# Adaptive-layernorm block in float32 on one core: summing eight factors in the DMA instead of on GpSimd, with a rearranged start

## The chip, the cores and the metric

The kernel runs on 1 core of one Trainium2 chip. The metric is device time in microseconds (us) of one execution; the median of three executions of the kernel before is 536.98 us (536.24 to 539.12). Engine names are those of the profile: PE is TensorE (PEld its weight loads), DVE is VectorE, ACT is ScalarE, POOL is GpSimd, SP is the sync engine, which here only issues DMAs.

## The reference, cut to what matters

Four batches `b` of 1024 tokens with 512 channels go through one attention block and one linear block, each behind a layer norm whose scale, shift and gate come from a small conditioning vector. All is float32.

```python
mod = (silu(c) @ wmod)            # 6 rows of 512 per batch: sa, ca, ga, sb, cb, gb
ga, gb = sign(.) * max(|.|, 0.25) of their rows
h = layernorm(x) * (1 + ca) + sa
# attention: every one of the 16 heads has the same scores, of rank 64
scores = (h Wq^T)(h Wk^T)^T;  attn = softmax(scores)
x = x + ga * ((attn @ (h Wv^T)) @ Wo^T)
h = layernorm(x) * (1 + cb) + sb
# the linear block: eight 512 x 512 factors act as their sum
x = x + gb * (h @ sum_r factors[r] / sqrt(8) + bias)
```

Since all heads share one attention matrix, the kernel multiplies the value and output weights into one matrix first (`wvo`), and since the linear block is linear in the factors, it sums the eight factors once (`fsum`).

## The kernel before, in words

**Stages.** For the first batch there is a start: load weights and tokens, multiply `wv` and `wo` into `wvo` (L172), make the modulation rows (L189), normalize the first batch's tokens and transpose them on PE (L375), and project queries and keys (L398, tile `ps_qk`). Then each batch runs: scores and `y = h·wvo·ga` alternating tile by tile (L425 and L478), the product of probabilities and `y` (L517), and, interleaved with the next batch, the linear block (L542). A batch has 8 token tiles of 128; `p` counts pairs of tiles, 4 a batch.

**The product.** Probabilities times `y` goes by a scheme with seven half-size products per pair (`n` = 1 to 7) in place of eight. It needs sums and differences of quarters of the transposed probabilities (`sum_probs`, L464, DVE) and of quarters of `y` (`sum_y`, L488; on DVE for batch 0). Each product of a pair is added into the residual tile `x` by one DVE instruction (`add`, L531), and products share PSUM banks: 1, 6, 7 and 4 accumulate in a bank `y` (two of these exist), 5 and 3 in `q`, 2 in `x`. So product 6, which goes on in the bank of product 1, cannot start before DVE has added product 1.

**Transposes.** Probabilities (128x2048 for a pair) are transposed in 32x32 blocks on DVE (`turn_probs`, L450, one instruction a pair), and 16 DMAs on SP's queue then move the blocks to their partitions (`move_probs`, L455, through `move_blocks`, L325). Normalized tokens go the same way (`turn_h`, `move_h`).

**Factors.** `fsum` receives factor 0 by two DMAs. Factors 1 to 7 are loaded in halves of 512 KB to one buffer of two halves (`load_factor`, L251) and added by POOL (`add_factor`, L267), 14 loads and 14 adds. POOL's queue issues both. POOL also computes reciprocal standard deviations (`rstd`, L300), parts of the second gate (L228), the scaled weights `w` of batches 1 to 3 (L276), the scaled `f` (L281), `sum_y` of batches 1 to 3, and it adds the bias rows to the residual (`add_bias`, L554). Stores of batches 0 to 2 and loads of the later batches' tokens are issued on its queue too.

**What sets the order.** A `Plan` (L17) holds every piece of work with a beat, written by hand; `pe(n, ...)` takes n beats of PE's time, `at(beat, ...)` puts other work beside it. Pieces are issued in order of beat, and each engine and queue runs its own list strictly in that order. A beat of the product stage is about 0.43 us: 112 beats there take 48 us. In the plan of batch 0, the score stage begins at beat 84, the product stage at 168, and the layer norm of batch 1's second half asks POOL for its standard deviations at beat 204.

**PSUM.** Eight banks: `y` has two tiles of one bank, `sc` two tiles of two banks, `q` and `x` one each. `psum_mm` (L91) hands out y, q, y, x in turn when no tag is given.

**First loads.** Before: the chunks of `wv`, the four first token tiles and the modulation weights go on SP's queue; `cT` (8 KB, the conditioning vector) and the four chunks of `woT` go on ACT's queue, `cT` first.

Of the kernel before, what the change touches and what calls it, by code (L numbers as in the profile page):

```python
# [12 lines left out]
ALU = mybir.AluOpType  # L13
# [3 lines left out]
class Plan:  # L17
# [6 lines left out]
    def at(self, beat, fn, *args):  # L24
        self.work.append((beat, len(self.work), fn, args))

    def pe(self, beats, fn, *args):
        self.at(self.now, fn, *args)
        self.now += beats
        return self.now  # L30
# [7 lines left out]
def kernel(  # L38
# [17 lines left out]
    nc = tc.nc  # L56
    P = 128
    B, T, D = x.shape
    NR = factors.shape[0]
    R = wqkT.shape[1] // 2  # L60
    KC = D // P
    NT = T // P
    NP = NT // 2
    GT = NT // 2
# [3 lines left out]
    NQ = P // Q  # L68
# [10 lines left out]
    wfp = ctx.enter_context(tc.tile_pool(name="wfp", bufs=2))  # L79
# [6 lines left out]
    def psum(tag, width, name):  # L86
        return psp.tile([P, width], F32, tag=tag, bufs=2 if tag in ("y", "sc") else 1, name=name)
# [3 lines left out]
    def psum_mm(name, tag=None):  # L91
        turn[0] += 1
        return psum(tag or "yqyx"[turn[0] % 4], 512, name)

    plan = Plan()
    at, pe = plan.at, plan.pe
# [15 lines left out]
    def load_x(b, t, queue=nc.sync):  # L112
        xt[b, t] = xp.tile([P, D], F32, tag="x", name=f"x_{b}_{t}")
        queue.dma_start(out=xt[b, t], in_=x[b, ts(t, P), :])

    def wide(pool, tag, name):
        return pool.tile([P, KC, D], F32, tag=tag, name=name)

    wvs, wos = wide(prp, "pr", "wvs"), wide(prp, "pr", "wos")
# [3 lines left out]
    def load_wmod(m):  # L123
        nc.sync.dma_start(
            out=wms[m], in_=wmod[:, ts(m, D)].rearrange("(kc p) e -> p kc e", p=P)
        )

    wqk = const.tile([P, KC, 2 * R], F32, name="wqk")
    cTs = const.tile([P, KC, B], F32, name="cTs")

    def load_weights(cc):
        nc.sync.dma_start(out=wvs[:, cc, :], in_=wv[ts(cc, P), :])
        nc.scalar.dma_start(out=wos[:, cc, :], in_=woT[ts(cc, P), :])

    for cc in range(KC - 1):
        load_weights(cc)
        load_x(0, cc)
        if cc == 0:
            nc.scalar.dma_start(out=cTs, in_=cT.rearrange("(kc p) b -> p kc b", p=P))
    load_x(0, KC - 1)  # L140
    load_wmod(0)
    load_wmod(1)
    load_weights(KC - 1)
# [20 lines left out]
    wvo = const.tile([P, KC, D], F32, name="wvo")  # L164
    pw = [psum("sc", T, f"ps_wvo_{h}") for h in range(2)]
# [6 lines left out]
    def wvo_chunk(cc, kcs=range(KC)):  # L172
        for kc in kcs:
            nc.tensor.matmul(  # L174
                pw[kc // 2][:, ts(kc % 2, 512)], wvs[:, cc, ts(kc, P)], wos[:, cc, :],
                start=(cc == 0), stop=(cc == KC - 1),
            )
        if cc == KC - 1:
            for kc in kcs:
                nc.scalar.copy(wvo[:, kc, :], pw[kc // 2][:, ts(kc % 2, 512)])  # L180

    row_tiles = [sp.tile([B, 3, D], F32, tag="s", name=f"rows_{h}") for h in range(2)]

    def row(m):
        return row_tiles[m // 3][:, m % 3, :]

    chans, rows_d, ps_mod = {}, {}, {}

    def mod_products(ms):  # L189
        ps = psum_mm(f"ps_mod_{ms[0]}", "q")  # L190
        for kc in range(KC):
            for g, m in enumerate(ms):
                nc.tensor.matmul(  # L193
                    ps[32 * g : 32 * g + B, :], scT[:, kc, :], wms[m][:, kc, :],
                    start=(kc == 0), stop=(kc == KC - 1),
                )
        for g, m in enumerate(ms):
            ps_mod[m] = ps[32 * g : 32 * g + B, :]
# [47 lines left out]
        nc.tensor.matmul(bcs["ga", 0], sel, row(2), start=True, stop=True)  # L246

    fsum = const.tile([P, KC, D], F32, name="fsum")
    fac = {}

    def load_factor(n):  # L251

        r, half = divmod(n, 2)
        if n == 0:
            fac["buffer"] = wide(wfp, "wf", "factors")
        f = fac["buffer"][:, ts(half, KC // 2), :]
        if r == 0:
            f = fsum[:, ts(half, KC // 2), :]
            nc.gpsimd.tensor_copy(f[0:1, 0, 0:1], chans[1][0:1, 0, 0:1])
        elif r == 1:  # L260
            nc.gpsimd.tensor_copy(f[0:1, 0, 0:1], chans[1][0:1, 0, 0:1])
        fac[n] = f
        nc.gpsimd.dma_start(
            out=f, in_=factors[r, ds(half * D // 2, D // 2)].rearrange("(kc p) e -> p kc e", p=P)
        )

    def add_factor(n):  # L267
        k = ts(n % 2, KC // 2)
        nc.gpsimd.tensor_tensor(fsum[:, k, :], fsum[:, k, :], fac[n], ALU.add)  # L269

    wb, fb = {}, {}

# [52 lines left out]
    def move_blocks(src, dst, apart, queue=nc.sync):  # L325

        if apart:
            src = src.rearrange("p (c n e) -> p c n e", c=NQ, e=Q)
            dst = dst.rearrange("p (n r e) -> p r n e", r=NQ, e=Q)
        else:  # L330
            src = src.rearrange("p (c w) -> p c w", c=NQ)
            dst = dst.rearrange("p (r w) -> p r w", r=NQ)
        for r in range(NQ):
            for c in range(NQ):
                queue.dma_start(out=dst[ts(c, Q), r], in_=src[ts(r, Q), c])  # L335

    def turn_h(ln, b, g, c):
# [57 lines left out]
    def project(b, g):  # L395
        if g == 0:
            qkT[b] = (
                qkp.tile([2 * R, T], F32, tag="qT", name=f"qT_{b}"),  # L398
                qkp.tile([2 * R, T // 2], F32, tag="kT", name=f"kT_{b}"),
            )  # L400
        ps = psum_mm(f"ps_qk_{b}_{g}")
        for kc in range(KC):
            nc.tensor.matmul(  # L403
                ps[: 2 * R, :].rearrange("p (r w) -> p r w", r=NQ), wqk[:, kc, :],
                h1_chunk(b, g, kc),
                start=(kc == 0), stop=(kc == KC - 1),
            )
        ps_qk[b, g] = ps
# [14 lines left out]
    probs, ps_sc, den, rinv, PT, S = {}, {}, {}, {}, {}, {}  # L423
# [23 lines left out]
            AF.Exp, bias=nm, scale=1.0, accum_out=den[b, p][:, k : k + 1],  # L447
        )

    def turn_probs(b, p):  # L450
        nc.vector.reciprocal(rinv[b][:, 2 * p : 2 * p + 2], den[b, p])  # L451
        v = probs[b, p].rearrange("p c k j e -> p (c k j e)")
        nc.vector.transpose(v, v)  # L453

    def move_probs(b, p):  # L455
# [103 lines left out]
    def plan_softmax(b, p, k):  # L559

        at(plan.now + 0.5, exponents, b, p, k)
        if k:
            at(plan.now + 7, turn_probs, b, p)
            at(plan.now + 8, move_probs, b, p)

    def plan_start():
        for g in range(2):
            s = 8.0 if g == 0 else 44.0
            for j in range(GT):
                at(s + 2 * j, stats, 1, 0, g * GT + j)  # L570
            at(s + 9, rstd, 1, 0, g)
            for j in range(GT):
                at(s + 10 + j, normalize_first, g * GT + j)
        pe(8, warm_up)
        for cc in range(KC - 1):
            pe(8, wvo_chunk, cc)
        pe(8, mod_products, [0, 1])
        at(plan.now, mod_row, 1, nc.vector)
        at(plan.now, mod_row, 0, nc.scalar)
        pe(4, wvo_chunk, KC - 1, range(2))  # L580
        for m, plus in ((1, 1.0), (0, 0.0)):
            pe(1, channel_products, m)
            at(plan.now, channel, m, plus)
        pe(4, wvo_chunk, KC - 1, range(2, KC))
        for kc in range(KC):
            pe(1, turn_first, 0, kc)
            at(plan.now, first_out, 0, kc)
        for n in range(2 * NR):
            at(plan.now + 10 * max(0, n - 3), load_factor, n)
            if n >= 2:  # L590
                at(plan.now + 10 * max(0, n - 1), add_factor, n)
        pe(8, project, 0, 0)
        at(plan.now, qk_out, 0, 0)
        for kc in range(KC):
            pe(1, turn_first, 1, kc)
            at(plan.now, first_out, 1, kc)
        pe(8, mod_products, [2, 3, 4, 5])
        at(plan.now, mod_row, 2, nc.vector)
        for m in (3, 4, 5):
            at(plan.now, mod_row, m, nc.scalar)  # L600
        at(plan.now, gate, 2)
        at(plan.now, publish, row(2), "ga")
        pe(8, project, 0, 1)
        at(plan.now, qk_out, 0, 1)
        pe(2, spread_first)
        for kc in range(KC):
            at(plan.now, scale_w, 0, kc, nc.vector)
# [43 lines left out]
    def plan_ln2(b, g, ready):  # L651

        for j in (GT - 2, GT - 1):
            at(ready, stats, 2, b, g * GT + j)
        at(ready + 0.5, rstd, 2, b, g)
        for j in range(GT):
            at(ready + 5 + 2 * j, normalize, 2, b, g, j, nc.vector)
        for c in range(NQ):
            at(ready + 13 + 2 * c, turn_h, 2, b, g, c)
        at(ready + 19.5, move_h, 2, b, g)  # L660
        for j in range(GT):
            at(ready + 16, add_bias, b, g * GT + j)
        for kc in range(KC):
            at(ready + 55, shift_h, 2, b, g, kc, nc.scalar)

# [92 lines left out]
```

## Time and profile before

| | before |
|---|---|
| median of 3 executions | 536.98 us (536.24 to 539.12) |
| profiled execution: time | 538.23 us |
| its span, first to last instruction | 536.4 us |
| PE idle in the span | 16.0 us (536.4 less 520.4 busy) |
| PE idle from 97.7 to 532.7 us | 0.07 us |
| DVE busy | 347.6 us, 65% of the span |
| POOL busy | 198.0 us, 37% |
| POOL's 14 factor adds (L269) | 33.4 us, 2388 ns each |
| POOL's 32 bias additions (L555) | 43.9 us, 1394 ns each |
| mean granted TensorE clock | 0.986 |
| HBM read, written | 28.33 MB, 8.41 MB |

The profiled execution is 1.25 us above the median; 1.83 us of its time lie outside its span. A row of the view by stages gives, for each stretch of time, the busy time and the number of instructions of PE, PEld, DVE, ACT and POOL, then the clock granted to TensorE (1.00 is full), the mean busy share of the 16 DMA engines, and GB/s. The share can pass 1, since a packet's time includes waiting. In a row of the timeline the two first numbers are start and duration in us; what stands in brackets is the idle time before the instruction and what ended it. L numbers are lines of the kernel.

### The profile page before, as it was taken

The page shows a single profiled execution, that of the slowest core. Times are in us where ns is not written, and L with a number is a line of the kernel's source. Part 1 is how long each engine was busy: PE and PEld are TensorE (multiplying, and loading weights), DVE is VectorE, ACT ScalarE, POOL GpSimd, SP SyncE. Part 2 cuts the span into 40 slices and gives each one's busy share as a digit, 9 for nine tenths or more (in the row PEclk, how much of TensorE's full clock was granted, in tenths as well). Part 3 has the DMA queues.
Part 4 walks back from the last instruction along what each step waited for, and adds up shares of the span by engine and source line. Part 5 has one row for each costly group of instructions (what it writes and reads, how often), then busy time and mean ns, then how long its engine had stood idle before and what let it go on. Part 6 is the DMA issues. An engine that isn't in the chain of part 4 may idle for free.

```text
span 536.4 us, 5575 instructions
## 1 busy us (share of the span) xinstructions
PE 520.4 (97%) x1738; PEld 306.6 (57%) x1738; DVE 347.6 (65%) x568; ACT 131.5 (25%) x206; POOL 198.0 (37%) x170
## 2 busy tenths in 40 slices
PE   8988998799999999999999999999999999999997
PEld 4343334688743344888743344888743348887442
DVE  3448699899765546689665545789665673784611
ACT  1133322212255410222155310232155310001020
POOL 1038487563144162243145072244144060450600
PEclk9997999799999999999999999999999999999999
DMA  9993589864537679523536679423536677005352
GB/s 321 381 388 116 146 156 216 139 132 106 77 51 106 93 138 227 166 69 79 78 50 104 98 148 226 155 64 80 78 50 110 96 130 139 6 5 76 102 134 78
DMA packets 223342, 68.60 MB, mean 128 GB/s; under 512 B 206528, under 2 KB 207040, under 8 KB 223312
## 3 DMA queue, kind: packets, MB, share of 16 engines
q1 hardware_dynamic: 216704, 48.30, 46.9%
q0 software_dynamic: 5504, 18.88, 10.9%
q10 hardware_dynamic: 1104, 1.06, 0.6%
q8 instruction: 14, 0.23, 0.2%
q14 instruction: 16, 0.13, 0.1%
HBM read 28.33 MB, written 8.41 MB: 68 GB/s over the span
## 4 chain that ended last, share of the span: by engine, by line
PE 88%; DVE 4%; SPq 2%; DMA 2%; ACT 2%; issue 1%; ACTq 0%; DVEq 0%
PE ps_o_y L526 21%; PE ps_f L545 20%; PE ps_y L483 17%; PE ps_o_q L526 10%; PE ps_sc L430 6%; PE ps_o_x L526 5%; PE ps_qk L403 5%; PE ps_wvo L174 3%; SPq L335 2%; PE ps_mod L193 1%; DMA wos<-in_woT_dram 1%; DMA pt<-pr 1%; DVE s L472 1%; DVE pr L453 1%; ACT hT L387 1%
## 5 line engine op out<-in xcount | busy, mean ns | idle before, releaser
L483 PE MATMUL ps_y<-w,hT 128*128 128x512 f32 x256 | 119.2, 609 | 0.0
L545 PE MATMUL ps_f<-f,hT 128*128 128x512 f32 x256 | 110.5, 592 | 0.0
L483 PEld LDWEIGHTS ps_y<-w,hT 128*128 128x128 f32 x256 | 46.8, 192 | 69.2 <-issue 67.6
L545 PEld LDWEIGHTS ps_f<-f,hT 128*128 128x128 f32 x256 | 48.6, 190 | 60.8 <-issue 59.6
L300 POOL TENSOR_TENSOR r<-v,mhalf 128x4 f32<-128x4 f32 x16 | 18.0, 1126 | 148.0 <-DVE v L298 130.9
L354 ACT ACTIVATE hT<-hT,chan,chan 128x512 f32<-128x512 f32 x56 | 41.0, 805 | 116.1 <-DMA hT<-st 116.1
L526 PE MATMUL ps_o_y<-y,pt 128*128 128x256 f32 x256 | 58.5, 379 | 0.0
L549 DVE TENSOR_TENSOR x<-ps_f,x 128x512 f32<-128x512 f32 x32 | 21.9, 685 | 50.7 <-PE ps_f L545 50.7
L526 PEld LDWEIGHTS ps_o_y<-y,pt 128*128 128x128 f32 x256 | 48.6, 190 | 8.3 <-issue 1.9
L293 DVE BATCH_NORM_STATS2 bn<-x 128x6 f32<-128x512 f32 x64 | 43.3, 677 | 6.7 <-DMA x<-in_x_dram 6.7
L555 POOL TENSOR_TENSOR x<-x,bc_gbias 128x512 f32<-128x512 f32 x32 | 43.9, 1394 | 6.1 <-DVE st L319 5.4
L317 ACT ACTIVATE st<-x,m,r 128x512 f32<-128x512 f32 x24 | 17.6, 803 | 112.1 <-DVE m L305 72.5
L443 DVE TENSOR_REDUCE nm<-ps_sc 128x1 f32<-128x1024 f32 x32 | 38.3, 1206 | 5.6 <-PE ps_sc L430 5.6
L534 DVE SCALAR_TENSOR_TENSOR x<-ps_o_y,ri,x 128x256 f32<-128x256 f32 x64 | 30.2, 471 | 17.6 <-PE ps_o_y L526 17.4
L281 POOL TENSOR_TENSOR f<-fsum,bc_gb 128x512 f32<-128x512 f32 x16 | 20.7, 1324 | 54.7 <-DMA bc_gb<-rows_gb 54.7
L444 ACT ACTIVATE pr<-ps_sc,nm 128x1024 f32<-128x1024 f32 x32 | 35.7, 1117 | 19.9 <-DVE nm L443 15.6
L339 DVE STREAM_TRANSPOSE st<-st 128x512 f32<-128x512 f32 x56 | 37.0, 689 | 5.5 <-ACT st L317 5.2
L430 PE MATMUL ps_sc<-kT,qT 64*128 64x512 f32 x128 | 38.8, 663 | 0.0
L453 DVE STREAM_TRANSPOSE pr<-pr 128x2048 f32<-128x2048 f32 x16 | 36.9, 2306 | 2.6 <-DMA pt<-pr 1.7
L269 POOL TENSOR_TENSOR fsum<-fsum,factors 128x1024 f32<-128x1024 f32 x14 | 33.4, 2388 | 11.7 <-DMA factors<-in_factors_dram 11.6
L526 PE MATMUL ps_o_y<-yt,s 128*128 128x256 f32 x128 | 32.1, 396 | 5.0 <-DVE x L534 5.0
L451 DVE RECIPROCAL ri<-den 128x2 f32<-128x2 f32 x16 | 2.6, 165 | 52.5 <-ACT pr L444 52.5
(81 smaller groups left out, 633.2 us busy)
## 6 DMA issues: line engine op xcount, KB each, us to landing
pt<-pr SPq DMA_DIRECT2D x256, 64.0 KB, 2.3
hT<-st SPq DMA_DIRECT2D x224, 64.0 KB, 2.2
factors<-in_factors_dram POOLq DMA_DIRECT2D x14, 512.0 KB, 5.1
wm<-in_wmod_dram SPq DMA_DIRECT2D x6, 1024.0 KB, 9.7
out_dram<-x POOLq DMA_DIRECT2D x24, 256.0 KB, 3.5
x<-in_x_dram SPq DMA_DIRECT2D x16, 256.0 KB, 8.9
x<-in_x_dram POOLq DMA_DIRECT2D x16, 256.0 KB, 4.6
out_dram<-x SPq DMA_DIRECT2D x8, 256.0 KB, 2.0
```

What stands on the lines that cost most here:

```text
L269: nc.gpsimd.tensor_tensor(fsum[:, k, :], fsum[:, k, :], fac[n], ALU.add)
L293: nc.vector.bn_stats(s, xt[b, t])
L339: nc.vector.transpose(s, s)
L354: eng.activation(v, v, AF.Identity, bias=shift, scale=scale)
L430: nc.tensor.matmul(ps_sc[b, i][:, ts(h, 512)], qT[h * R : (h + 1) * R, ts(i, P)], kT[h * R : (h + 1) * R, :], start=True, stop=True,)
L443: nc.vector.tensor_reduce(nm, ps_sc[b, i], AX.X, ALU.max, negate=True)
L444: nc.scalar.activation(probs[b, p][:, :, k].rearrange("p c j e -> p j c e"), ps_sc[b, i].rearrange("p (j c e) -> p j c e", j=NT, c=NQ), AF ...
L453: nc.vector.transpose(v, v)
L483: nc.tensor.matmul(ps, h_rows(1, b, t, kc), wb[b][:, kc, :], start=(kc == 0), stop=(kc == KC - 1))
L526: nc.tensor.matmul(ps, a[:, ts(j, P)], bb[:, j, :], start=(tag is not None and j == 0), stop=(j == GT - 1), skip_group_check=tag is None,)
L545: nc.tensor.matmul(ps, h_rows(2, b, t, kc), fb[b][:, kc, :], start=(kc == 0), stop=(kc == KC - 1))
L555: nc.gpsimd.tensor_tensor(xt[b, t], xt[b, t], bcs["gbias", b], ALU.add)
```

## The change

- **Factors.** The eight factors go into `fsum` by eight DMAs of 1 MB on POOL's queue; the first writes, the other seven add to what is there. Each waits for the one before, since they write one tile. The buffer, the 16 half loads and the 14 POOL adds are gone. The eight are issued at beats 54, 78, ... 222 in place of 54 to 194.
- **Bias additions** move from 16 beats after the second layer norm's ready point to 76 and 36 beats after it (24 in the last batch), 4 beats apart: for batches 0 to 2 they fall into the next batch's score stretch.
- **First loads.** All `wv` and `wo` chunks go on SP's queue; the first four token tiles go on ACT's, with `cT` behind them.
- **PSUM and weight copies.** The first batch's projection uses `sc` tiles; the products of modulation rows 2 to 5 use a `y` tile, not `q`. Copies of `wvo` out of PSUM are placed singly; the last two come behind the first layer-norm copies on ACT's list. As `psum_mm` is called without a tag less often, the turn of the later tiles moves by two.
- **Turnings in pieces.** `turn_probs` transposes a pair in four pieces of 128x512, 1.6 beats apart, and `move_blocks` issues its 16 DMAs piece by piece. `move_probs` stands 12 beats after the scores in place of 8.

```diff
     def load_weights(cc):
         nc.sync.dma_start(out=wvs[:, cc, :], in_=wv[ts(cc, P), :])
-        nc.scalar.dma_start(out=wos[:, cc, :], in_=woT[ts(cc, P), :])
+        nc.sync.dma_start(out=wos[:, cc, :], in_=woT[ts(cc, P), :])
     for cc in range(KC - 1):
         load_weights(cc)
-        load_x(0, cc)
-        if cc == 0:
-            nc.scalar.dma_start(out=cTs, in_=cT.rearrange("(kc p) b -> p kc b", p=P))
-    load_x(0, KC - 1)
+        load_x(0, cc, nc.scalar)
+    load_x(0, KC - 1, nc.scalar)
+    nc.scalar.dma_start(out=cTs, in_=cT.rearrange("(kc p) b -> p kc b", p=P))
...
-        if cc == KC - 1:
-            for kc in kcs:
-                nc.scalar.copy(wvo[:, kc, :], pw[kc // 2][:, ts(kc % 2, 512)])
+    def wvo_out(kc):
+        nc.scalar.copy(wvo[:, kc, :], pw[kc // 2][:, ts(kc % 2, 512)])
...
-    def load_factor(n):
...
-    def add_factor(n):
-        k = ts(n % 2, KC // 2)
-        nc.gpsimd.tensor_tensor(fsum[:, k, :], fsum[:, k, :], fac[n], ALU.add)
+    def sum_factor(r):
+        if r == 0:
+            nc.gpsimd.tensor_copy(fsum[0:1, 0, 0:1], chans[1][0:1, 0, 0:1])
+        nc.gpsimd.dma_start(
+            out=fsum, in_=factors[r].rearrange("(kc p) e -> p kc e", p=P),
+            accum_op=ALU.bypass if r == 0 else ALU.add,
+        )
...
-        for r in range(NQ):
-            for c in range(NQ):
+        for c in range(NQ):
+            for r in range(NQ):
                 queue.dma_start(out=dst[ts(c, Q), r], in_=src[ts(r, Q), c])
...
-        ps = psum_mm(f"ps_qk_{b}_{g}")
+        ps = psum_mm(f"ps_qk_{b}_{g}") if b else psum("sc", T, f"ps_qk_{b}_{g}")[:, :512]
...
-    def turn_probs(b, p):
-        nc.vector.reciprocal(rinv[b][:, 2 * p : 2 * p + 2], den[b, p])
-        v = probs[b, p].rearrange("p c k j e -> p (c k j e)")
+    def turn_probs(b, p, c):
+        if c == 0:
+            nc.vector.reciprocal(rinv[b][:, 2 * p : 2 * p + 2], den[b, p])
+        v = probs[b, p][:, c].rearrange("p k j e -> p (k j e)")
         nc.vector.transpose(v, v)
...
-            at(plan.now + 7, turn_probs, b, p)
-            at(plan.now + 8, move_probs, b, p)
+            for c in range(NQ):
+                at(plan.now + 7 + 1.6 * c, turn_probs, b, p, c)
+            at(plan.now + 12, move_probs, b, p)
...
+        at(plan.now, wvo_out, 2)
+        at(plan.now, wvo_out, 3)
+        for r in range(NR):
+            at(plan.now + 24 * r, sum_factor, r)
...
-        pe(8, mod_products, [2, 3, 4, 5])
+        pe(8, mod_products, [2, 3, 4, 5], "y")
...
-            at(ready + 16, add_bias, b, g * GT + j)
+            at(ready + (24 if b + 1 == B else 76 if g == 0 else 36) + 4 * j, add_bias, b, g * GT + j)
```

More of the change, by code (lines that the diff above doesn't have):

```diff
@@ L187, with mod_products @@
     chans, rows_d, ps_mod = {}, {}, {}
-    def mod_products(ms):
-        ps = psum_mm(f"ps_mod_{ms[0]}", "q")
+    def mod_products(ms, tag):
+        ps = psum_mm(f"ps_mod_{ms[0]}", tag)
         for kc in range(KC):
@@ L248 @@
     fsum = const.tile([P, KC, D], F32, name="fsum")
-    fac = {}
-    def load_factor(n):
[L253 to L256, printed above, removed]
-        if r == 0:
[L258 to L262, printed above, removed]
+    def sum_factor(r):
+        if r == 0:
+            nc.gpsimd.tensor_copy(fsum[0:1, 0, 0:1], chans[1][0:1, 0, 0:1])
         nc.gpsimd.dma_start(
-            out=f, in_=factors[r, ds(half * D // 2, D // 2)].rearrange("(kc p) e -> p kc e", p=P)
-        )
-    def add_factor(n):
-        k = ts(n % 2, KC // 2)
-        nc.gpsimd.tensor_tensor(fsum[:, k, :], fsum[:, k, :], fac[n], ALU.add)
+            out=fsum, in_=factors[r].rearrange("(kc p) e -> p kc e", p=P),
+            accum_op=ALU.bypass if r == 0 else ALU.add,
+        )
     wb, fb = {}, {}
@@ L576, in plan_start @@
             pe(8, wvo_chunk, cc)
-        pe(8, mod_products, [0, 1])
+        pe(8, mod_products, [0, 1], "q")
         at(plan.now, mod_row, 1, nc.vector)
@@ L580, in plan_start @@
         pe(4, wvo_chunk, KC - 1, range(2))
+        at(plan.now, wvo_out, 0)
+        at(plan.now, wvo_out, 1)
         for m, plus in ((1, 1.0), (0, 0.0)):
@@ L587, in plan_start @@
             at(plan.now, first_out, 0, kc)
[L588 to L591, printed above, removed]
+        at(plan.now, wvo_out, 2)
+        at(plan.now, wvo_out, 3)
+        for r in range(NR):
+            at(plan.now + 24 * r, sum_factor, r)
         pe(8, project, 0, 0)
```

## The prediction, on record before the result

> **What bounds the kernel now.** I read the page's first part, then the busy time by stages cut where PE's idle time changes, then the waits and the chain that ended last, then the timeline of 38 to 98 us. PE is busy in 97% of the span, so the question is where the other 16.0 us lie. The view by stages (start:end, then length, busy PE, PEld, DVE, ACT, POOL, clock, DMA share, GB/s):
>
> ```profile
> 18.50:29.50 11.00, 9.85 (x49) 4.40 (x48) 5.76 (x15) 4.15 (x7) 1.10 (x2) 1.00 1.05 386
> 29.50:46.50 17.00, 13.92 (x66) 5.71 (x66) 9.49 (x13) 4.84 (x9) 8.08 (x11) 1.00 0.73 271
> 46.50:56.30 9.80, 9.80 (x19) 3.31 (x18) 6.38 (x10) 1.93 (x4) 8.85 (x7) 0.65 0.44 155
> 56.30:88.40 32.10, 32.10 (x89) 12.72 (x90) 28.31 (x35) 10.89 (x19) 21.02 (x15) 1.00 0.85 166
> 88.40:97.70 9.30, 3.90 (x18) 2.79 (x16) 9.30 (x15) 1.68 (x3) 2.90 (x2) 0.85 1.12 192
> 97.70:532.70 435.00, 434.93 (x1472) 269.97 (x1472) 281.24 (x462) 106.48 (x164) 154.35 (x130) 1.00 0.53 103
> ```
>
> From 97.7 us on PE never waits, at full clock: nothing done there to DVE, POOL or SP can save time. All that can be won lies before 97.7 us, and the largest piece is the stretch from 88.4, where DVE is busy all 9.30 us and PE 3.90. The waits name it:
>
> ```profile
> PE ps_o_y L526 <- DVE x L534: 5.0, 1, 5.0
> ```
>
> Product 6 waits for DVE's addition of product 1. The timeline shows why DVE is late (start, length, engine, line):
>
> ```profile
> 84.84 2.33 POOL L269 TENSOR_TENSOR fsum<-fsum,factors 128x1024 f32<-128x1024 f32 x1 [0.55 <-DMA factors<-in_factors_dram]
> 84.90 2.83 DVE L472 TENSOR_TENSOR s<-pt 128x512 f32<-128x512 f32 x1 [0.19 <-DMA pt<-pr]
> ...
> 88.21 2.36 POOL L269 TENSOR_TENSOR fsum<-fsum,factors 128x1024 f32<-128x1024 f32 x1
> ...
> 88.78 2.08 DVE L499 TENSOR_TENSOR yt<-y,yt 128x256 f32<-128x256 f32 x1
> ...
> 91.46 0.68 DVE L472 TENSOR_TENSOR s<-s,pt 128x512 f32<-128x512 f32 x1
> ```
>
> The same DVE instruction takes 2.83 us when a POOL factor add is running and 0.68 us when none is: it ends just after POOL's add ends. DVE stands still while POOL adds.
>
> **Part 1, the POOL adds go.** In the stretch before the addition of product 1, four DVE instructions run into POOL adds: 128x1024 at 78.49 (2.04 us, POOL until 79.44: 0.85 lost), 128x256 at 80.97 (2.58 against 0.41: 2.17), 128x512 at 84.90 (2.83 against 0.68: 2.15), 128x256 at 88.78 (2.08 against 0.41: 1.67). Sum 6.8 us. The wait is 5.04; it goes if DVE keeps pace. What is then late next is PE itself: DVE's addition would come near 97.12 - 6.8 = 90.3, and product 5 ends at 92.6. PE's clock also fell in that wait: product 6 took 3.78 us against 1.73 for its kind later, 2.05 more, and the next 0.2 more. Value -7.2, from 0 (something else holds DVE) to -7.2.
>
> Earlier, the gate's instruction L221 takes 2.45 us at 42.27, beside a POOL add from 41.84 to 44.45, and 0.41 at 65.20, without one. It is on the chain: row 2, gate, `ps_ga`, where PE waits 1.47. With 2.04 off, PE's own projection is last there: -1.47. The clock of 0.65 in 46.5 to 56.3 follows that gap: eight `ps_y` records take 5.02 us there against 3.70 later, 1.3 more, and the eight `ps_sc` 4.79 against 2.30 in batch 1, of which 1.5 is the wait for `scale_w`, which stays, so 1.0 more. I take -1.5 of the 2.3, since one gap of three stays; bounds 0 to -2.3.
>
> **Part 2, banks.** PE waits 0.87 before the first projection (bank q, until ACT has copied the fourth transposed chunk), 0.67 before a transpose (bank q again, L421), 0.87 before the modulation products (again). Other banks are free there: -2.4. The limit is the modulation weights: the last of six 1 MB loads is issued at 18.1 and lands 13.5 later, at 31.6; with parts 2 and 3 it is wanted at 36.78 - 2.4 - 1.5 = 32.9. So the cover is 1.3 us; without it part 2 is 0. A changed turn gives product 5 bank q without the wait for `y`'s copy: -0.36.
>
> **Part 3, first loads.** PE's warm-up ends at 5.00 and the first `wvo` product starts at 6.41, when the first `wo` chunk lands (1.23 + 5.05 on ACT's queue). In front of it there sits `cT`, which ACT had only at 3.94 although it has 8 KB. The first token tile, issued at 1.18 behind one 256 KB chunk on SP's queue, landed by 4.34. That is the place that `wo` gets, but it now shares the engines with token tiles. Lower end: it lands as the second `wv` chunk did (1.65 + 5.1 = 6.76 for the third in the queue, so no gain). Upper end: 1.41 and the 1.7 us that four cold records at 0.85 cost over 0.43, -3.1. Value -1.5, nearer to the token tile's row.
>
> **Part 4, pieces.** A 128x2048 turning takes 2.31 us; two 128x512 together 1.29 in `turn_h`, so four cost 2.6: +0.3 a pair, 1.2 before the addition, inside the 2.3 us by which DVE is early (92.6 - 90.3). The first moves can start after one piece, 1.6 us sooner (0.69 against 2.31); they are issued at 0.67 us each alone (10.80 for 16), 0.80 beside factor loads (38.54 for 48).
>
> **Part 5, bias additions.** 32 POOL instructions of 1.39 us leave the product stage (DVE 34.4 of 40 us busy in 220:260) for the score stage (23.1 of 40 in 260:300). PE has no idle time in either: 0. The cover is DVE's 17 idle us per 40. In POOL's list they stand around `scale_f`, which waits 13.96 us for its broadcast row and ends at 173.5; `ps_f` begins at 189.1. Bounds 0.
>
> **Part 6, the new wait.** POOL blocks at each summing DMA until the one before has landed. Behind it stand, for batch 0: the second gate (and through it two SP DMAs, ahead of pair 1's moves), and `rstd` for batch 1 at beats 171 and 204, the latter behind the seventh sum. The profile has no such DMA. Low bound: a half load alone, 3.6 us. High: four half loads one after another at the slowest under moves, 4 x 6.0 = 24 us, since each 1 MB must also be read where it is added. I take 12: two half loads under moves are 10.4 (2 x 5.2), plus something for the second read. Condition: before, the second `rstd` at 114.02 was 24.2 us ahead of the finished shift at 138.25, and the projection took that at 148.2. With PE 14.5 earlier, `rstd` may come at 148.2 - 14.5 - 24.2 = 109.5. The fourth sum is held to about 62 by the gate, so the seventh goes out at 62 + 3D: at D = 12, 98, and 0 cost. From D = 16 PE waits; from 20.5 the whole gain is gone.
>
> The Trainium skill ("Collectives: The Full Stack", The bandwidth ceiling) says that a DMA which adds reads two sources and reached about half the rate of a copy. No run here shows it yet; applied to the 5.2 row it gives about 2 x 2 x 3.2 + 2 = 15 us, an estimate, and the sum stays as it is.
>
> The same skill ("SBUF — State Buffer", Two separate sides) speaks against DMAs from POOL: DVE's two-port modes keep POOL from writing descriptors. The trace does not show it for the factor loads: 14 issues at 0.72 to 0.78 us, most beside a busy DVE. By the rule each sum might start up to a DVE instruction later; the sum above has no term for it.
>
> **Give-back.** SP's moves now set when DVE can form `sum_probs`. With PE 6.9 earlier at the first exponents, SP starts near 52; pair 0 ends near 64; at 0.80 each pair 2 lands near 64 + 25.6 + 4.4 = 94 against a need near 92, pair 3 near 107 against 104. DVE runs in order, so its additions wait a little: +2 (0 to +6).
>
> **Sum.** -7.2 - 1.5 - 1.5 - 2.4 - 0.4 - 1.5 + 2 = -12.5 from 538.23: 525.7; from the median, 1.25 lower, 524.5. I say 525. All favourable ends: -7.2 - 1.5 - 2.3 - 2.4 - 0.4 - 3.1 = -16.9, 520 from the median.
>
> **Rivals.** (a) *Moves late.* Each 0.1 us more per move issue is 4.8 us on pair 3. At 0.90 the give-back is 2 + 5: about 531. For: the DMA share is already 1.12 there. Against: the sums come one at a time, with gaps. (b) *The gain given back whole*: at 1.05 per issue, 12 us, 537, no change. (c) *Slower: the sums take too long.* At D = 24 the seventh goes out at 134, 25 us past 109.5: 525 + 25 = 550. It decides from D = 20.5. For: nothing in the profile excludes it; against: the half loads' 3.6 to 6.0 us.
>
> **Chances.** Forecast 0.62, (a) 0.20, (b) 0.07, (c) 0.11. About 0.5% (2.7 us) is what a measurement of this kernel tells from no change: faster 0.82, same 0.07, slower 0.11. The range 520 to 533 holds the forecast with its bounds and (a).
>
> **What would show it.** No POOL adds, and 128x512 and 128x256 sums on DVE at 0.68 and 0.41 from 75 to 95; the wait of `ps_o_y` on DVE under 1; clock 1.00 in that stretch; `wvo` starting near 5; the sums landing within 16 us. A wait of PE on `ps_qk` near 135, or of DVE on `pt` near 95, would make the prediction wrong.

## The result, and the profile after

The changed kernel takes 553.1 us (median of four, 548.3 to 553.6) against 536.6 for the kernel before on the same chip: a ratio of 1.028 (95% interval 1.021 to 1.035). It is slower; 525 was predicted, with a range of 520 to 533. The profiled execution took 553.6 us, with a span of 551.8 and a mean clock of 0.978.

The view by stages of the changed kernel, with the same columns as before (start:end, length, busy PE, PEld, DVE, ACT, POOL, clock, DMA share, GB/s):

```profile
46.50:56.30 9.80, 9.80 (x21) 3.98 (x20) 4.11 (x8) 2.84 (x5) 1.29 (x1) 0.77 0.67 115
88.40:97.70 9.30, 6.39 (x22) 5.34 (x23) 5.42 (x14) 2.93 (x4) 2.68 (x2) 0.82 0.62 88
110.00:120.00 10.00, 10.00 (x48) 8.81 (x47) 5.70 (x14) 2.93 (x4) 1.50 (x2) 1.00 0.99 161
120.00:130.00 10.00, 2.62 (x9) 1.89 (x8) 2.87 (x5) 0.00 (x0) 1.20 (x1) 0.80 0.92 171
```

From 88.4 to 97.7 us PE now works 6.39 us instead of 3.90, as intended. But from 120 to 130 us, where it had no idle time before, it stands for 7.4 of 10 us, and DVE is idle there as well (2.87 busy). Only the DMA engines are busy (0.92). The waits of the changed kernel (us in total, times, longest) name what is late:

```profile
POOL fsum L253 <- DMA fsum<-in_factors_dram: 39.1, 5, 9.9
DVE s L460 <- DMA pt<-pr: 18.0, 4, 10.3
PE ps_o_q L514 <- DVE x L522: 8.1, 2, 7.4
PE ps_sc L417 <- ACT kT L408: 6.0, 4, 2.9
PE ps_o_y L514 <- DVE x L522: 3.2, 1, 3.2
```

DVE waits 18.0 us for moves of probabilities (before: 0.2), and PE waits for DVE's additions, which stand behind those sums in DVE's list. A second, smaller loss is the wait of PE for `kT`: 6.0 us in four places. The timeline shows the moves themselves, 16 for the first pair and 48 for the other three:

```profile
55.13 10.86 SPq L322 DMA_DIRECT2D pt<-pr  x16
67.06 57.37 SPq L322 DMA_DIRECT2D pt<-pr  x48
124.47 0.62 SPq L239 DMA_DIRECT2D bc_ga<-rows_ga  x1
```

The 48 issues take 57.37 us, 1.195 each, where the kernel before needed 38.54, 0.80 each. They end at 124.4, and the broadcast of the next batch's gate (`bc_ga`) goes out only behind them, at 124.47 (111.04 before). DVE's sums for the second, third and fourth pair and PE's longest wait, in the same view:

```profile
90.17 0.69 DVE L460 TENSOR_TENSOR s<-pt 128x512 f32<-128x512 f32 x1 [3.60 <-DMA pt<-pr]
106.30 0.69 DVE L460 TENSOR_TENSOR s<-pt 128x512 f32<-128x512 f32 x1 [3.88 <-DMA pt<-pr]
127.13 0.69 DVE L460 TENSOR_TENSOR s<-pt 128x512 f32<-128x512 f32 x1 [10.29 <-DMA pt<-pr]
128.27 3.78 PE L514 MATMUL ps_o_q<-y,s 128*128 128x256 f32 x8 [7.38 <-DVE x L522]
```

Each pair is later than the one before it: 3.6, 3.9, 10.3 us of idle DVE. The brackets of the last two rows are the chain: moves, sum, addition, product.

Where the time came from is read at the start of `ps_f` in each batch: 200.4, 322.4 and 444.4 us against 189.1, 309.2 and 429.4 before. So 11.3 us are lost up to the first `ps_f`, the change to batch 1 included, and about 1.9 more at each of the two next changes of batch; the span is 15.4 longer.

**The bias additions.** The rows around the change to batch 2, first of the changed kernel, then of the kernel before:

```profile
279.72 5.49 POOL L543 TENSOR_TENSOR x<-x,bc_gbias 128x512 f32<-128x512 f32 x4
279.79 2.88 DVE L306 TENSOR_SCALAR st<-x,mv,r 128x512 f32<-128x512 f32 x2 [1.21 <-POOL r L287]
282.59 0.68 DVE L406 COPY qT<-ps_qk 64x512 f32<-64x512 f32 x1
288.65 1.98 PE L417 MATMUL ps_sc<-kT,qT 64*128 64x512 f32 x6 [1.07 <-ACT kT L408]
```

```profile
268.49 1.00 DVE L319 TENSOR_SCALAR st<-x,mv,r 128x512 f32<-128x512 f32 x2 [1.22 <-POOL r L300]
269.12 5.57 POOL L555 TENSOR_TENSOR x<-x,bc_gbias 128x512 f32<-128x512 f32 x4 [0.66 <-DVE st L319]
269.41 0.68 DVE L419 COPY qT<-ps_qk 64x512 f32<-64x512 f32 x1
```

Before, the four additions waited for the two normalizations (`st`), since they change the tile that `st` reads. Moved to later beats they are additions of another half, which wait for nothing. POOL starts them directly behind `rstd`, together with the first `st`. Two `st` then take 2.88 us instead of 1.00, the copy of the queries comes 1.9 us later, and PE waits.

**What came as predicted.** The first `wvo` product starts at 5.53 us (6.41 before); the bank waits and the 1.47 us before `ps_ga` are gone. DVE's sums take 0.68 us where they met an addition before:

```profile
81.08 0.68 DVE L460 TENSOR_TENSOR s<-s,pt 128x512 f32<-128x512 f32 x1
```

**What did not.** The row from 46.5 to 56.3 us shows a clock of 0.77 (0.65 before), but the first scores now start at 42.8 us instead of 46.5. In the 9.8 us from there, 42.8 to 52.6, the clock is 0.65 as before. Product 6 still waits 3.2 us for DVE, now because DVE waits for moves (90.17) and not because POOL adds.

### The profile page after: what moved, and what is told of

The parts are those of the page before. It is cut to its first block, busy times and chain, and to the rows that moved or that the text cites. A ratio compares the mean times of both kernels' runs of the same rounds, so it can differ in the third digit from the quotient of the medians.

```text
span 551.8 us, 5646 instructions
## 1 busy us (share of the span) xinstructions
PE 527.7 (96%) x1738; PEld 308.3 (56%) x1738; DVE 337.1 (61%) x616; ACT 130.7 (24%) x206; POOL 160.0 (29%) x145
## 3 DMA queue, kind: packets, MB, share of 16 engines
q1 hardware_dynamic: 216704, 48.30, 44.9%
q0 software_dynamic: 7168, 18.88, 14.5%
q10 hardware_dynamic: 1104, 1.06, 0.6%
## 4 chain that ended last, share of the span: by engine, by line
PE 83%; DVE 5%; SPq 4%; DMA 3%; ACT 1%; POOL 1%; issue 1%; DVEq 0%; POOLq 0%; ACTq 0%
PE ps_f L533 20%; PE ps_y L471 19%; PE ps_o_y L514 17%; PE ps_o_q L514 9%; PE ps_sc L417 6%; PE ps_o_x L514 4%; SPq L322 4%; PE ps_wvo L173 3%; DVE st L306 2%; PE ps_mod L192 1%; PE ps_qk L390 1%; DMA pt<-pr 1%; POOL w L263 1%; DMA wos<-in_woT_dram 1%; DMA bc_ga<-rows_ga 1%
## 5 line engine op out<-in xcount | busy, mean ns | idle before, releaser
L471 PE MATMUL ps_y<-w,hT 128*128 128x512 f32 x256 | 121.9, 621 | 0.0
L417 PE MATMUL ps_sc<-kT,qT 64*128 64x512 f32 x128 | 41.1, 673 | 6.5 <-ACT kT L408 6.0
L441 DVE STREAM_TRANSPOSE pr<-pr 128x512 f32<-128x512 f32 x64 | 41.5, 685 | 2.6 <-DMA pt<-pr 1.2
L543 POOL TENSOR_TENSOR x<-x,bc_gbias 128x512 f32<-128x512 f32 x32 | 41.8, 1333 | 1.1 <-DVE st L306 1.0
L514 PE MATMUL ps_o_q<-y,s 128*128 128x256 f32 x128 | 32.1, 396 | 7.4 <-DVE x L522 7.4
L474 ACT COPY y<-ps_y 128x512 f32<-128x512 f32 x32 | 18.7, 585 | 75.0 <-PE ps_y L471 74.9
## 6 DMA issues: line engine op xcount, KB each, us to landing
wm<-in_wmod_dram SPq DMA_DIRECT2D x6, 1024.0 KB, 10.7
```

Source lines behind the costliest of these rows:

```text
L417: nc.tensor.matmul(ps_sc[b, i][:, ts(h, 512)], qT[h * R : (h + 1) * R, ts(i, P)], kT[h * R : (h + 1) * R, :], start=True, stop=True,)
L471: nc.tensor.matmul(ps, h_rows(1, b, t, kc), wb[b][:, kc, :], start=(kc == 0), stop=(kc == KC - 1))
L514: nc.tensor.matmul(ps, a[:, ts(j, P)], bb[:, j, :], start=(tag is not None and j == 0), stop=(j == GT - 1), skip_group_check=tag is None,)
L543: nc.gpsimd.tensor_tensor(xt[b, t], xt[b, t], bcs["gbias", b], ALU.add)
```

## Experiments

Theories at the start: **1**, the summing DMAs slow SP's moves, and this is nearly the whole loss; **2**, moving the bias additions loses it; **3**, the start, the banks or the pieces do. Each time is the median of a kernel; the ratio is to the kernel before, which took 536.3 to 536.8 us beside these runs, and its 95% interval stands in brackets.

**undo_sums**: the changed kernel with the factors as before (half loads, POOL adds).

```diff
-        for r in range(NR):
-            at(plan.now + 24 * r, sum_factor, r)
+        for n in range(2 * NR):
+            at(plan.now + 10 * max(0, n - 3), load_factor, n)
+            if n >= 2:
+                at(plan.now + 10 * max(0, n - 1), add_factor, n)
```

> The changed kernel with the factors summed as before: half loads and POOL adds, all other parts of the change kept. Theory 1 (a summing DMA in flight keeps the small moves of the probabilities off the DMA engines, 1.0 to 2.0 us per issue against 0.63): the 48 moves of pairs 1 to 3 come back to about 0.80 us each, DVE's waits for pt (18.0 us) nearly vanish, and the time falls to 531 to 540 us. Rival 2 (the bias additions cost it): still above 545. Rival 3 (turning in pieces and the later moves cost it): still above 545.

538.2 us, ratio 1.0037 (1.0016 to 1.0059). The moves are back to 0.80 us each, and DVE's waits for them are gone:

```profile
65.44 38.53 SPq L335 DMA_DIRECT2D pt<-pr  x48
```

The sums account for most of the loss. But this kernel has the start, banks and pieces and still gains nothing: something else costs several microseconds.

**undo_bias**: the changed kernel with the bias additions where they were.

```diff
-            at(ready + (24 if b + 1 == B else 76 if g == 0 else 36) + 4 * j, add_bias, b, g * GT + j)
+            at(ready + 16, add_bias, b, g * GT + j)
```

> The changed kernel with the bias additions back at 16 beats after the ready point, one beat for all four. Theory 1: 545 to 550 us, since at each of three batch boundaries POOL's first additions hold DVE's normalizing (2.88 us against 1.00) before the copy of the queries; the rest of the loss stays. Rival 2: back to 540 or less.

546.8 us, 1.018 (1.015 to 1.022), 6.3 below the changed kernel. DVE's waits for the moves stay, 17.3 us.

**before_sums**: the kernel before, with the summing DMAs alone.

> The kernel before with only the factors summed by accumulating DMAs. Theory 1: slower by 6 to 16 us than before (543 to 553), with moves at 1.2 us each over pairs 1 to 3, although DVE meets no POOL adds. Rivals 2 and 3: no slower than before, 530 to 537.

549.2 us, 1.022 (1.017 to 1.026): 12.9 us lost by the sums alone. Timeline and waits show the same picture, 1.10 us a move:

```profile
71.75 52.71 SPq L322 DMA_DIRECT2D pt<-pr  x48
```

```profile
DVE s L459 <- DMA pt<-pr: 17.7, 4, 8.7
```

**plain_1mb**: is it the size of the DMAs or the adding?

```diff
-            accum_op=ALU.bypass if r == 0 else ALU.add,
+            accum_op=ALU.bypass,
```

> The changed kernel with all eight DMAs writing in place of adding, so fsum holds the last factor alone: same bytes from HBM, same waits of POOL, no read of the target. If it is the adding that fills the DMA engines: each lands in 5 to 8 us in place of 9.7, moves at 0.75 to 0.9 us, time 533 to 542. If it is 1 MB at a time from POOL's queue that does it: 548 to 553, moves unchanged.

540.9 us, 1.0065 (1.0028 to 1.0102), 12.1 below the changed kernel. Its executions lie between 537.1 and 544.0; the profiled one took 538.2. The page's row of DMA issues (KB each, median us to landing) for the changed kernel and for this one, and the moves of this one:

```profile
fsum<-in_factors_dram POOLq DMA_DIRECT2D x8, 1024.0 KB, 9.7
```

```profile
fsum<-in_factors_dram POOLq DMA_DIRECT2D x8, 1024.0 KB, 6.6
```

```profile
61.80 45.68 SPq L322 DMA_DIRECT2D pt<-pr  x48
```

With the same queue, order and bytes, a DMA that adds lands in 9.7 us and one that overwrites in 6.6 (medians). The 48 moves, gaps between the big DMAs included, take 1.195 us each beside the one and 0.95 beside the other (0.75 to 0.9 had been expected; 0.80 beside the half loads). So most of the price is the adding: 12.1 of the 14.9 us between undo_sums and the changed kernel. Moves beside plain DMAs of 1 MB are slowed too. Smaller adding DMAs were not tried. The part of the page on queues shows what the adding takes (packets, MB, share of 16 engines over the span); POOL's queue, changed kernel first:

```profile
q0 software_dynamic: 7168, 18.88, 14.5%
```

```profile
q0 software_dynamic: 5376, 18.88, 10.7%
```

14.5% of 551.8 us are 80.0 us of all 16 engines, 10.7% of 536.4 are 57.4. The bytes are equal, but seven adding DMAs bring 1792 more packets, 256 each, and 22.6 us more of engine time, 3.2 each. The other kernels agree: 58.5 to 59.7 us in before, undo_sums and undo_both, 79.8 to 81.1 in before_sums, undo_bias and sums_late. The packets of SP's queue, which holds the moves, took no more than here: 44.9% of the span or 248 us in the changed kernel, 46.9% or 252 us in this one. The 48 moves were 18.8 us longer than in undo_sums. A packet's time includes waiting, so these sums show where the engines' time went, not how an engine works inside.

**undo_both**: sums and bias additions as before; start, banks and pieces as changed.

> The changed kernel with the factors summed on POOL as before and the bias additions at their old place; what stays is the rearranged start, the banks and the turning in pieces. Theory 1 with the bias as the second cause: about 530 to 533 us, 4 to 6 below before, since product 6 of pair 0 starts 6.5 us sooner with the sums undone, and nothing later gives it back. If the turning in pieces costs something: 534 to 538.

530.6 us, 0.990 (0.988 to 0.992). Theory 3 falls: these parts gain 6 us. So from 530.6 the bias move alone costs 7.6 (undo_sums, 538.2), the sums alone 16.2 (undo_bias, 546.8), both 22.5 (553.1). The price of the sums is a net one: what DVE gains without POOL's adds is already in it. The old wait of product 6 is still there with POOL adding, 5.2 us (5.0 before):

```profile
PE ps_o_y L527 <- DVE x L535: 5.2, 1, 5.2
```

**start_only**: undo_both with one turning a pair and the old order of the moves.

```diff
-            for c in range(NQ):
-                at(plan.now + 7 + 1.6 * c, turn_probs, b, p, c)
-            at(plan.now + 12, move_probs, b, p)
+            at(plan.now + 7, turn_probs, b, p)
+            at(plan.now + 8, move_probs, b, p)
```

> As undo_both, and the turning in one piece with the moves in their old order: the start and the banks alone. If the pieces gain nothing on PE's path: the same as undo_both within 1.5 us. If they cost: 2 to 4 us faster than undo_both.

532.7 us, 0.993 (0.991 to 0.995). Start and banks give about 4 us. The pieces seem to give 2, neither nothing nor a cost as the expectation had it; but the intervals of the two kernels overlap, so this gain is not shown. Without pieces the first move goes out at 53.0 instead of 51.5, and the wait of product 6 is 6.8 instead of 5.2.

**bias_late**: undo_sums, with the additions placed behind `scale_f` in POOL's list.

```diff
-            at(ready + (24 if b + 1 == B else 76 if g == 0 else 36) + 4 * j, add_bias, b, g * GT + j)
+            at(ready + (24 if b + 1 == B else 90 if g == 0 else 42), add_bias, b, g * GT + j)
```

> As undo_sums, with the bias additions of batches 0 to 2 behind scale_f in POOL's list, which waits 14 us for its row: they then run in the score stretch. If the cost of the bias part (538.2 against 530.6) is that POOL runs them at once, beside DVE's normalizing: back to 529.5 to 532. If additions in the score stretch cost by themselves: 536 to 539.

531.4 us, 0.990 (0.988 to 0.993): the whole 7 us are back, though the additions lie even later. The waits and timeline of undo_sums, then those of bias_late:

```profile
PE ps_sc L430 <- ACT kT L421: 4.1, 4, 1.1
```

```profile
142.35 5.50 POOL L556 TENSOR_TENSOR x<-x,bc_gbias 128x512 f32<-128x512 f32 x4
142.42 2.89 DVE L319 TENSOR_SCALAR st<-x,mv,r 128x512 f32<-128x512 f32 x2 [1.21 <-POOL r L300]
```

```profile
PE ps_sc L430 <- ACT kT L421: 0.9, 1, 0.9
```

```profile
140.29 1.00 DVE L319 TENSOR_SCALAR st<-x,mv,r 128x512 f32<-128x512 f32 x2 [1.21 <-DMA hT<-st]
163.76 9.85 POOL L556 TENSOR_TENSOR x<-x,bc_gbias 128x512 f32<-128x512 f32 x8
```

So the score stage can carry the additions, as the prediction had it. Their place behind `rstd` was the cost. At batch 1 the two score tiles around the wait take from 149.10 to 153.21 in undo_sums and the same eight products in undo_both 146.97 to 149.20: 1.9 us more, three times 5.7. The other 2.1 us of the two profiled spans' difference lie before that place. Of these, 1.5 are there at product 6 of batch 0 already (91.15 us against 89.70), ahead of any bias addition. So the profiles show 5.7 us of the move's cost; what makes up the rest of the 7.6 stays open.

**small_adds**: the kernel before with POOL adding 32 of 1024 columns, to price the adds by themselves.

> The kernel before with each POOL add on 32 of its 1024 columns only: the factor sum is left out but for those; loads, waits and order stay. It prices what DVE loses to the adds alone. By the reading of the profile of before: product 6 waits under 1 us, L221 takes 0.41 us, and the time is 526 to 531 us. If DVE was late for other reasons: 535 or more.

531.2 us, 0.990 (0.988 to 0.992): the adds cost 5.6 us, not the 8.7 that the prediction took for them (7.2 and 1.5). Product 6 waits 3.1 us, where under 1 had been expected. The waits show what is late next:

```profile
PE ps_o_y L526 <- DVE x L534: 3.1, 1, 3.1
...
DVE s L472 <- DMA pt<-pr: 4.7, 3, 3.7
```

**moved_adds** and **adds_clear**: undo_both with the POOL adds (and the loads behind them) placed so that few meet DVE's work: seven (moved_adds) or five (adds_clear) ahead of the gate, the next three or four behind it, the rest behind the layer norm of batch 1. The diff is that of adds_clear.

```diff
-            at(plan.now + 10 * max(0, n - 3), load_factor, n)
+            beat = plan.now + (10 * max(0, n - 1) if n < 7 else 60 + 8 * (n - 7) if n < 11 else 120 + 8 * (n - 11))
...
+                at(beat, add_factor, n)
```

> As undo_both, with the POOL adds moved in the list: adds 2 to 8 ahead of the gate, 9 to 11 behind it, 12 to 15 behind the standard deviations of batch 1's first half, so that no add meets DVE's sums between 78 and 92 us. If DVE standing still at POOL's adds is what made product 6 late: its wait of 5.2 us falls below 2 and the time to 524 to 529 us. If something else holds DVE: as undo_both.

530.4 us, 0.988 (0.986 to 0.991): not told apart from undo_both, and above the 524 to 529 expected. The wait of product 6 is gone (0.3 us are left on a later product), but adds now met the gate, and PE waited there instead:

```profile
61.08 2.77 DVE L220 TENSOR_SCALAR rows<-rows 4x512 f32<-4x512 f32 x1
61.21 2.35 POOL L269 TENSOR_TENSOR fsum<-fsum,factors 128x1024 f32<-128x1024 f32 x1
```

```profile
PE ps_ch L205 <- DVE chan L210: 2.6, 2, 1.7
```

> As moved_adds, with adds 2 to 6 ahead of the gate, 7 to 10 behind it and 11 to 15 behind the standard deviations of batch 1's first half: in moved_adds two adds met the gate on DVE (L220 took 2.77 us) and PE waited 2.6 us for the channel columns instead. If DVE standing still at POOL's adds is all that was left of the stall: no wait of PE on DVE above 1 us after 46 us, and 523 to 527 us. If DVE is simply full: again 529 to 531.

528.9 us, 0.985 (0.982 to 0.988): 1.7 us below undo_both, with intervals that just touch, and 2 us above the 523 to 527 expected. Product 6 still waits 1.5 us (5.2 in undo_both).

**clear_bias_late**: adds_clear and bias_late together.

> adds_clear and bias_late together, the candidate for the best version: the same as adds_clear within 1.5 us, since the product stage has no idle time on PE to win; slower than adds_clear by 2 or more if additions in the score stretch hold anything up.

528.5 us, 0.985 (0.983 to 0.988): the lowest median of this study, 1.5% under the kernel before, with the factors summed on POOL. It can't be told from adds_clear; the late bias additions add nothing to that.

**sums_late**: undo_bias with sums 3 to 7 behind the second half's `rstd` of batch 1, so that few sums fly beside the 48 moves.

```diff
-            at(plan.now + 24 * r, sum_factor, r)
+            at(plan.now + (24 * r if r < 3 else (151, 152, 175, 182, 228)[r - 3]), sum_factor, r)
```

> As undo_bias, with summing DMAs 3 to 7 behind the standard deviations of batch 1's second half, so that they fly beside the moves of the normalized tokens and not beside those of the probabilities. Theory 1: the probabilities' 48 moves go at 0.63 to 0.68 us each, DVE's waits for pt fall under 3 us and product 6 waits under 1; the token moves take over the slowness (1.2 to 1.5 us each), PE waits for the projections of batch 1, and the time is 538 to 555. If the probabilities' moves stay at 1 us or more, theory 1 is wrong.

543.2 us, 1.010 (1.006 to 1.014); its executions scatter from 537.4 to 547.1. The profile is of one near the lower end, 537.6, so its rows don't explain the whole of the median. The moves of the probabilities are the fastest of all, 0.72 us each, and DVE's sums hardly wait for them any more (0.2 us). But the 64 token moves behind them now take 0.95 us each (0.80 before; 1.2 to 1.5 had been expected), and POOL's list has a new wait. Timeline and waits:

```profile
67.22 34.38 SPq L322 DMA_DIRECT2D pt<-pr  x48
102.86 60.48 SPq L322 DMA_DIRECT2D hT<-st  x64
...
125.71 1.31 POOL L253 DMA_DIRECT2D fsum<-in_factors_dram  x1 [3.74 <-DMA fsum<-in_factors_dram]
126.53 1.55 POOL L287 TENSOR_TENSOR r<-v,mhalf 128x4 f32<-128x4 f32 x1
128.11 0.55 DVE L306 TENSOR_SCALAR st<-x,mv,r 128x512 f32<-128x512 f32 x1 [5.12 <-POOL r L287]
```

```profile
PE ps_o_q L514 <- DVE x L522: 8.0, 1, 8.0
```

A sum waits on POOL until the one before it has landed, the next `rstd` stands behind it, DVE waits 5.12 us for `rstd`, an addition of the product stands behind that on DVE, and PE waits 8.0 us. What the probabilities' moves gained, the tokens' moves and POOL's list gave back. An estimate shows how tight the stretch is: in the changed kernel six of the eight sums go out behind 49 us and are in flight for some 58 us (8.9 to 10.5 each), the 128 moves of batch 0 take 81 at the 0.63 us of an undisturbed one, and both lie in some 110 us (50 to 160). Within it some moves must fly beside a sum. That no order of the sums helps is not shown; other orders were not tried.

## Why the prediction was wrong

**The failed term: the give-back of SP's moves, +2 (0 to +6).** It kept 0.80 us per move, the price beside half loads of which at most a few are under way. With a sum in flight single issues took 0.6 to 2.8 us, in most stretches of 5 us 1.0 to 2.0 in the median, and a move landed 3.1 to 9.6 us after its issue. In the one gap without, 86 to 94 us, when POOL waited for the next `rstd`, the issues took 0.63 and the moves landed after 2.1 to 2.8. The mean of the 48 issues was 1.195. By rival (a)'s own rule, 4.8 us on pair 3 for each 0.1 us, that is 19 us, and the 48 moves did end 18.8 us later than at undo_sums' pace. The measured price of the sums is 16.2 us (undo_both to undo_bias), net of what DVE gains. The prediction had named the sign itself, a wait of DVE on `pt` near 95 us: DVE waited 3.60 us before 90.17, 3.88 before 106.30 and 10.29 before 127.13. The chain of rival (a) was right and its price was not: it stopped at 0.90, with the reason that "the sums come one at a time, with gaps", and (b) at 1.05. There were hardly any gaps: a sum was under way for 48 of the 57 us.

The term looked at how long a sum would last, but not at what it takes from others while it lasts. Part 6 bounded the landing generously (12 us; it was 8.9 to 10.5) and asked only whether POOL waits too long. It doesn't: `rstd` ran at 109.14, 0.4 us before the time it was given. So rival (c) did not happen in this kernel, though its 550 is near the measured time; a near number from a wrong mechanism. Its chain shows in sums_late, where the sums are placed otherwise. The data to price the other side was partly there: the DMA share of the kernel before was already 1.12 in a part of the stretch in which the sums were to fly.

The Trainium skill ("Collectives: The Full Stack", The bandwidth ceiling: the fold count and why AG ≠ RS ≠ AR) gives the adding step of a collective about half the rate of the copying one, because it reads two sources. Here it is 6.6 / 9.7 = 0.68 of it. The prediction applied the rule to the sum's own landing alone; it had no term for the engines' time, of which an adding DMA took 3.2 us of all 16 engines more than a plain one. The skill ("DMA: Bandwidth & Descriptors", Queues, rings and completion order) says that an engine turns from queue to queue after whole packets; the slower moves agree with such sharing, but no run here shows the order of packets.

**The second failed term: the bias additions at 0.** The plan's beats were read as times. They only give an order: POOL runs its list as soon as it can. DVE's 17 idle us per 40 were true and beside the point, because the additions ran at the one moment when DVE's next instruction was on PE's path. They cost 7.6 us by undo_sums against undo_both, 6.3 by the changed kernel against undo_bias. As a rough reckoning, the predicted 525 with the 19 us of the moves and these 7.6 in place of nothing comes to 552; 553.1 was measured. The Trainium skill ("SBUF — State Buffer", Who interferes with whom) says that of two instructions that need the port pair which DVE shares with GpSimd, the second to start is blocked entirely; two `st` that start 0.07 us behind a POOL addition and take 2.88 us in place of 1.00 agree.

**DVE's relief: right in kind, too large.** POOL adds do hold up DVE, and without them the sums took 0.68. But 7.2 + 1.5 was the price with nothing late behind it; small_adds shows 5.6, since the moves were next (4.7 us of waits of DVE on `pt`). In the changed kernel product 6 began at 91.3 instead of 97.7; the prediction had put PE 14.5 us earlier there, at 83. The 1.47 us before `ps_ga` were put down to the wrong part: start_only and undo_both have POOL's adds and have lost this wait too, since the rearranged start brings the gate ahead of the first add (in start_only its instruction starts at 36.96 and takes 0.41 us, the add starts at 39.73).

**Start, banks, pieces: right in sum, partly by luck.** First loads, banks and the changed turn were put at -1.5 - 2.4 - 0.4 = -4.3; start_only, which has these alone, gained 4.0 (536.7 to 532.7). That gain also holds the 1.47 us before `ps_ga`, and against it product 6 waits 6.8 us there in place of 5.0. The first `wvo` product gained 0.9 us of the 1.4 that the wait for `wo` had been. One profile can't price the rest of the first loads: the first 24 `wvo` products took 12.78 us in the profile of the changed kernel and 10.54 in those of start_only, undo_sums and undo_both, which load in the same way, and with the old loads 12.11 in before and 10.54 in before_sums. The pieces, which the prediction put at no gain, gave at most some 2. The clock's term did not come in the changed kernel (0.65 in the 9.8 us from its first scores); start_only has 0.83 there, and why they differ stays open.

**The range.** It was said to hold the forecast with its bounds, but it did not: with part 1's -7.2 at 0 and the give-back at +6, both bounds of the prediction's own, its sum is 536 and not 533.

## What to carry to other kernels

Before work moves from an engine to the DMA engines, add up the time that the DMAs already need in that stretch, and price the change by what the other queues lose, not by how long the new DMA takes. When an instruction is moved in a list, look at which instruction it will stand behind and what runs on the other engine at that moment: a list runs as early as it can, and a dependency that goes away can be what held it in a harmless place.

## What was not expected of the hardware

- In the changed kernel an adding DMA of 1 MB lands in 8.9 to 10.5 us, those that fly ahead of the moves included (9.1 and 9.3), while the moves stretch from 0.63 to as much as 2.8 us per issue. One in sums_late took 12.8. A plain one lands in 6.6 (median).
- 64 KB moves on one queue cost per issue 0.63 us alone; on average over the 48 moves 0.77 to 0.83 beside half loads that wait for POOL's full adds (0.86 in small_adds, where the adds are short), 0.95 beside plain loads of 1 MB, 1.06 to 1.20 beside adding ones.
- Seven adding DMAs had 1792 more packets and some 22 us more time of all 16 engines than the same bytes copied.
- POOL's additions hold up DVE's normalizations too, not its sums alone: two 128x512 took 2.88 us in place of 1.00.
